# One buffer and four transfers for the queries of a unit, in place of three pieces and twelve

## The chip, the cores and the metric

The kernel runs on one core of a Trainium2 chip. The metric is the time of one launch in microseconds on the device, and the time of a version is the median of its runs. The core has five engines with an instruction queue each: TensorE (PE in the profile; its weight loads are PEld), VectorE (DVE), ScalarE (ACT), GpSimd (POOL) and SyncE (SP), which here only issues transfers (DMAs). An engine works through its own queue strictly in order, and engines wait for each other on semaphores.

## The reference

Two cross attention layers are applied one after the other to 32 sequences of 256 positions with 320 channels, with 77 context rows of 512 channels for each sequence. There are 20 heads of 16 channels. Cut to what is computed:

```python
def layer(x, ctx, Wq, Wk, Wv, Wo, bo):         # all float32
    q, k, v = heads(x @ Wq), heads(ctx @ Wk), heads(ctx @ Wv)
    s = einsum("bhqd,bhkd->bhqk", q, k) / sqrt(16)
    o = merge(einsum("bhqk,bhkd->bhqd", softmax(s), v))
    return o @ Wo + bo + x

x = layer(x, ctx, *L0)       # the object, others and ip parts of layer 0 have no rows here
x = layer(x, ctx, *L1)
```

## The kernel before

**Units.** Sixteen pairs of sequences times two layers make 32 units, in an order in which layer 0 runs four pairs ahead of layer 1 (`units_in_order`). Channels lie on partitions and positions along the free axis, so a pair's 320 x 512 values are 1280 columns (NX) of 128 partitions. The 20 heads of the two sequences form five groups of 256 columns; groups 0 to 3 are columns 0 to 1023, group 4 is the rest.

**What a unit does.** `keys` and `queries` (or `outputs_and_queries`, which also makes the outputs of the unit three before) project with TensorE; ScalarE copies the results to SBUF as `kR` and `q`. `mask_keys` makes `kT`. `maxima` computes scores once in order to find each row's maximum (TensorE writes `psm` at L500, VectorE reduces it at L512); `turn` lays these maxima out as rows, and SyncE moves them to `max_rows` (L537). `scores` computes the scores again, transposed, for the exponential: at L550 it puts the negative maxima into PSUM (`pss`), and at L558 it adds keys times queries. For accuracy these use a high and a low half of each number, made by `split` (L278 is the high half, L279 the low one). `products` and `divide` multiply with the values and normalise (`po` L578, `turned` L590, `normal` L599 on GpSimd), `turn_back` makes `oT`.

**The queries' halves.** The scores need the two heads of a pair on all partitions, and the high and low half of a head on neighbouring ones. `split_queries(u, i)` splits piece i of `q` into a buffer `halves`; `spread_queries(u, i)` moves it to `qs` with four DMAs (L316), one for each head e of a pair and each half h, each from 64 partitions to 64 others. The pieces are columns 0 to 511 (groups 0 and 1), 512 to 1023 (groups 2 and 3) and 1024 to 1279 (group 4); the `halves` tag has two buffers of 2 x 512 columns. So a unit has twelve such DMAs: eight of 128 KB and four of 64 KB. Unit 0 is split on VectorE, all others on GpSimd.

**Order.** The order is written out by hand. `at(slot, where, step)` files every step, and at the end the slots are gone through in order, and in each slot the places in a fixed order:

```python
order = (
    "load", "maxima", "turn back", "scores", "values", "rest", "back", "turn", "split", "full", "last",
)
```

`start(u)` is unit u's slot: 0, 5, 9, 13 and then the same 17 later, and so on. Unit u's first scores (group 0) stand in slot `start(u)`, except that the last unit's stand in `start(30) + 3`. Its pieces are split in slots `start(u-1) - 1`, `start(u-1)` and `start(u-1) + 1`, and spread at the head of `start(u-1)`, `start(u-1) + 1` and `start(u-1) + 2`. Every DMA but a few of the first weights is issued by SyncE in this order: loads of x (L120), contexts (L125, L426) and weights (L140), kS from `k_halves` (L290), v from `stage` (L480, L485), `max_rows` (L537), and the stores (L624, L643). A SyncE that waits for one of them holds all that follow.

**Buffers.** `ident`, a 128 x 128 identity, is a constant of its own; it is read once, at L178. `turned` has two buffers of 544 columns.

Of the kernel before, what the change touches and what calls it, by code (L numbers as in the profile page):

```python
# [52 lines left out]
F32 = mybir.dt.float32  # L53
F32R = mybir.dt.float32r
# [4 lines left out]
B, S, C, CA, L = 32, 256, 320, 512, 77  # L59
HEADS, HD = 20, 16  # L60
P = 128
NB = 2
NT = NB * S
NX = 2 * NT + S
# [31 lines left out]
def xattn_kernel(ctx: ExitStack, tc: tile.TileContext, xT, cT, cP, weights, outT):  # L96
    nc = tc.nc

    const = ctx.enter_context(tc.tile_pool(name="const", bufs=1))
    io = ctx.enter_context(tc.tile_pool(name="io", bufs=3))  # L100
    work = ctx.enter_context(tc.tile_pool(name="work", bufs=3))
# [11 lines left out]
    def load_x(p):  # L113
        x_sb = io.tile([P, NX], F32, tag="x", name=f"x_{p}", bufs=AHEAD + 2)
        xs[p] = x_sb
        if p == 0:
            for a, b in ((0, NT), (NT, 2 * NT), (2 * NT, NX)):
                nc.sync.dma_start(out=x_sb[:, a:b], in_=xT[p, :, a:b])
        else:
            (nc.scalar if p == 1 else nc.sync).dma_start(out=x_sb, in_=xT[p])  # L120

    def load_context(u):
        p = units[u][0]
        c_sb = cs[u] = io.tile([P, NKA, NB * L], F32, tag="c", name=f"c_{u}", bufs=3)
        nc.sync.dma_start(out=c_sb, in_=cP[:, p])  # L125
# [3 lines left out]
    for layer in range(2):  # L129
        wide = const.tile([P, WIDE], F32, name=f"w_{layer}")  # L130
        d = {"all": wide}
# [12 lines left out]
    first, _, _ = PARTS["q"]  # L144
    for i in range(2):
        n = slice(first + i * C, first + (i + 1) * C)
# [4 lines left out]

    ones = const.tile([P, P], F32, name="ones")
    nc.vector.memset(ones, 1.0)
    ident = const.tile([P, P], F32, name="ident")
    make_identity(nc, ident)


# [37 lines left out]
    st = [{} for _ in units]  # L195
# [80 lines left out]
    def split(engine, high, low, x):  # L276

        engine.tensor_copy(high, x)  # L278
        engine.tensor_tensor(low, x, high.bitcast(F32), ALU.subtract)  # L279

    def split_keys(u):

        split(nc.gpsimd if u else nc.vector, k_halves[:, :, 0], k_halves[:, :, 1], st[u].pop("kr"))
# [11 lines left out]
    PIECES = ((0, NT), (NT, 2 * NT), (2 * NT, NX))  # L295

    def split_queries(u, i):

        a, b = PIECES[i]
        x = st[u]["halves", i] = work.tile(  # L300
            [P, 2, NT], F32R, tag="halves", name=f"halves_{u}_{i}", bufs=2
        )
        split(
            nc.gpsimd if u else nc.vector, x[:, 0, : b - a], x[:, 1, : b - a], st[u]["q"][:, a:b]
        )

    def spread_queries(u, i):

        a, b = PIECES[i]
        if i == 0:  # L310
            st[u]["qs"] = work.tile([P, 2, NX], F32R, tag="qs", name=f"qs_{u}", bufs=2)
        to = st[u]["qs"].bitcast(F32).rearrange("(d h) e n -> h e d n", h=2)
        x = st[u].pop(("halves", i)).bitcast(F32).rearrange("(d e) h n -> e h d n", e=2)
        for e in range(2):
            for h in range(2):
                nc.sync.dma_start(out=to[h, e, :, a:b], in_=x[e, h, :, : b - a])  # L316

    def keys(u, t):
        p, layer = units[u]
        w, c_sb = w_sb[layer], cs[u]  # L320
        if t == 0:
            st[u]["kr"] = work.tile([P, NG, L], F32, tag="kR", name=f"kR_{u}", bufs=2)
        kR = st[u]["kr"]
        ps = bank(f"psk_{u}_{t}")
        for kc in range(NKA):
            by_columns(
                ps[:, 0 : 2 * L],
                w["k"][:, kc, t * P : (t + 1) * P],
                c_sb[:, kc, :],
                start=(kc == 0),  # L330
                stop=(kc == NKA - 1),
            )
        nc.scalar.copy(kR[:, 2 * t : 2 * t + 2].rearrange("p g k -> p (g k)"), ps[:, 0 : 2 * L])  # L333
        mask_keys(u, t)

    def keys_rest(u):

        p, layer = units[u]
        w, c_sb = w_sb[layer], cs[u]
        ps = bank(f"psk_{u}_2")  # L340
        for kc in range(NKA):
            for i in range(4):
                b, m = 1 - i // 2, i % 2
                nc.tensor.matmul(  # L344
                    ps[32 * i : 32 * i + 32, 0:L],
                    w["k"][:, kc, 2 * P + 32 * m : 2 * P + 32 * m + 32],
                    c_sb[:, kc, b * L : (b + 1) * L],
                    start=(kc == 0),
                    stop=(kc == NKA - 1),
                )  # L350
        nc.scalar.copy(st[u]["kr"][:, 4], ps[:, 0:L])
        mask_keys(u, 2)
# [70 lines left out]
    def load_chunk(layer, i):  # L423
        n = min(P, B * L - i * P)
        c_sb = cvs[layer, i] = io.tile([P, NKA, P], F32, tag="cv", name=f"cv_{layer}_{i}", bufs=3)
        nc.sync.dma_start(out=c_sb[:, :, :n], in_=cT[:, :, i * P : i * P + n])  # L426
# [180 lines left out]
    def values(u, g):  # L607
        st[u]["n", g] = divide(u, g, products(u, g))
# [47 lines left out]
    def at(slot, where, step):  # L656
        place.setdefault((slot, where), []).append(step)

    def start(u):

        return 17 * (u // 4) + (0, 5, 9, 13)[u % 4]
# [17 lines left out]
    for u, (p, layer) in enumerate(units):  # L679

        s = start(u - 2)
        if layer == 0 and u > 0:
            at(s - 5 - (u == 1), "load", lambda p=p: load_x(p))
        if u > 0:
            at(s - 4, "load", lambda u=u: load_context(u))
        if u > 1:
            k = (0, 1, 2) if u == 2 else (s - 2, s - 1, s + 1)
            at(k[0], "rest", lambda u=u: keys(u, 0))
            at(k[1], "rest", lambda u=u: keys(u, 1))
            at(k[2], "rest", lambda u=u: keys_rest(u))  # L690
        paired = u > 2 and u - 3 not in late
        if paired:
            at(s, "full", lambda u=u: outputs_and_queries(u - 3, u))
        elif u > 1:
            at(s, "last", lambda u=u: queries(u))
        if u > 1:
            at(s + 2, "split", lambda u=u: split_keys(u))
            at(start(u - 1), "load", lambda u=u: spread_keys(u))
            for i in range(3):
                at(start(u - 1) + i - 1, "split", lambda u=u, i=i: split_queries(u, i))  # L700
                at(start(u - 1) + i, "load", lambda u=u, i=i: spread_queries(u, i))
        need = range(p * NB * L // P, ((p + 1) * NB * L - 1) // P + 1)
        new = [i for i in need if i >= made[layer]]
        made[layer] += len(new)
        first = (-6, -2)[u] if u < 2 else start(u - 1) + 1
        slots = {}
        for k, i in enumerate(new):
            at(first - 3 - (u == 0) + k, "load", lambda layer=layer, i=i: load_chunk(layer, i))
            if i in few:
                slots[i] = first  # L710
                at(first, "full", lambda layer=layer, i=i: vals_of_few(layer, i))
                continue
            for h in range(2):
                slots[i] = first + (0 if u < 2 else k if len(new) > 1 else h)
                at(slots[i], "full", lambda layer=layer, i=i, h=h: vals(layer, i, h))
        for i in need:
            at(slots.get(i, first), "full", lambda u=u, i=i: place_vals(u, i))
        for g in range(NG):
            slot = slot_of(u, g)
            at(slot, "scores", lambda u=u, g=g: scores(u, g))  # L720
            at(slot + 1, "values", lambda u=u, g=g: values(u, g))
            if g < 4:
                at(slot + 2, "turn back", lambda u=u, g=g: turn_back(u, g))
            else:
                at(slot + 1, "back", lambda u=u, g=g: turn_back(u, g))
        if u == NU - 1:
            at(end, "full", lambda u=u: finish(u))
            at(end, "last", lambda u=u: finish_rest(u))
        if u in late:
            for t in range(2):  # L730
                at(late[u][t], "full", lambda u=u, t=t: finish(u, (t,)))
            at(late[u][2], "rest", lambda u=u: finish_rest(u))
            at(max(late[u]), "last", lambda u=u: store(u))
# [32 lines left out]
    at(-7, "split", lambda: split_keys(0))  # L766
    at(-6, "load", lambda: spread_keys(0))
    for i in range(3):
        at(-6 + i, "split", lambda i=i: split_queries(0, i))
        at(-5 + i, "load", lambda i=i: spread_queries(0, i))  # L770
    for slot, h, n in ((-6, 0, 3), (-6, 3, 3), (-4, 6, 2), (-4, 8, 2)):
        at(slot, "maxima", lambda h=h, n=n: maxima((0, h, n)))
    at(-4, "turn", lambda: turn(0))
# [1 line left out]
    at(-3, "split", lambda: split_keys(1))  # L775
    at(-2, "load", lambda: spread_keys(1))
    for i in range(3):
        at(-3 + i, "split", lambda i=i: split_queries(1, i))
        at(-2 + i, "load", lambda i=i: spread_queries(1, i))
    for slot, h, n in ((-2, 0, 3), (-2, 3, 2), (0, 5, 3)):  # L780
        at(slot, "maxima", lambda h=h, n=n: maxima((1, h, n)))
    at(1, "maxima", lambda: maxima((1, 8, 2), (2, 0, 1)))
# [118 lines left out]
```

## Time and profile before

| | |
|---|---|
| time, median of three runs | 944.42 us (943.32 to 945.34) |
| the profiled execution | 947.08 us, of which 945.3 us are the span of the instructions |
| busy: PE, PEld, DVE, ACT, POOL | 926.6, 640.8, 574.5, 432.0, 406.9 us |
| granted TensorE clock, mean | 0.998 |
| chain that ended last | PE 88%, DVE 7%, DMA 2%, SPq 1%, issue 1% |
| DMA packets | 114740, 133.03 MB |
| spread of the queries | 256 DMAs of 128 KB and 128 of 64 KB, median issue 587 ns |
| splits of the queries on GpSimd | high half 606 ns, low half 1277 ns for 512 columns |

A busy time is the union of an engine's instructions; PE includes what the model of the profile takes for the ends of its pipelined matmuls. A row of the waits names the engine and line that waited, who ended the wait, the total in us, the number of times and the longest. A row of the timeline has the start and the length in us, the engine, the line, the operation, what it writes and reads, and how many instructions were merged. SPq is SyncE's queue: the time there is that of issuing a DMA, not of moving its data. A row of the busy times by stretch has, for each engine, us and instructions, and at the end the granted clock of TensorE as a share, the mean share of the 16 DMA engines that was busy, and GB/s.

### The profile page before, as it was taken

Reading aid. Unit: us, or ns where it says so; the run is one execution under the profiler, and the core shown is the slowest. Engines: PE = TensorE matmul, PEld = TensorE weight load, DVE = VectorE, ACT = ScalarE, POOL = GpSimd, SP = SyncE. Lnnn points to the kernel's source line nnn. Section 1 sums busy time; section 2 is a strip of 40 time slices with the busy share of each in tenths; the row PEclk is TensorE's granted clock in tenths of the full one; section 3 lists DMA queues with packets and bytes.
Section 4 is the critical chain, followed back from the end, with each engine's and each line's share of the span. In section 5 each row is a group of like instructions: output and inputs, shape, how many; then the busy total and the mean of one; then the engine's idle time right before and its main releaser. Section 6 shows DMA issues by size and latency. Waiting matters only on the chain.

```text
span 945.3 us, 48848 instructions
## 1 busy us (share of the span) xinstructions
PE 926.6 (98%) x21582; PEld 640.8 (68%) x21582; DVE 574.5 (61%) x1330; ACT 432.0 (46%) x975; POOL 406.9 (43%) x608
## 2 busy tenths in 40 slices
PE   8999999999999999999999999999999999999998
PEld 6666667766667666666766677666767666676654
DVE  4475557655577565665656666665566654776575
ACT  2254443644435534355443545335454354444462
POOL 2354445434455434455234454344553335543431
PEclk9999999999999999999999999999999999999999
DMA  6664444253453525536245352355433543353342
GB/s 227 196 217 129 133 147 145 82 172 120 163 153 95 197 76 163 165 104 201 68 145 176 98 201 82 125 175 161 153 96 120 160 155 119 92 162 105 118 136 97
DMA packets 114740, 133.03 MB, mean 141 GB/s; under 512 B 47012, under 2 KB 76004, under 8 KB 114530
## 3 DMA queue, kind: packets, MB, share of 16 engines
q1 hardware_dynamic: 113666, 127.42, 42.8%
q8 instruction: 170, 2.79, 1.3%
q10 hardware_dynamic: 864, 2.49, 0.7%
q14 instruction: 40, 0.33, 0.1%
HBM read 35.39 MB, written 10.49 MB: 49 GB/s over the span
## 4 chain that ended last, share of the span: by engine, by line
PE 88%; DVE 7%; DMA 2%; SPq 1%; issue 1%; POOL 0%; ACT 0%; POOLq 0%
PE psy L203 15%; PE po L578 15%; PE psq L203 14%; PE psm L500 10%; PE psv L203 7%; PE pss L558 7%; PE psk L203 7%; PE psy L237 4%; PE pss L550 4%; PE psq L237 3%; DVE m L512 3%; DVE turned L590 1%; PE psk L344 1%; DVE maxes L533 1%; SPq L316 1%; DMA x<-in_xT_dram 1%
## 5 line engine op out<-in xcount | busy, mean ns | idle before, releaser
L564 ACT ACTIVATE pT<-pss 77x512 f32<-77x512 f32 x640 | 324.4, 593 | 171.7 <-PE pss L558 171.0
L512 DVE TENSOR_REDUCE m<-psm 128x6 f32<-128x462 f32 (+2 forms) x512 | 248.3, 551 | 221.4 <-PE psm L500 220.9
L599 POOL TENSOR_TENSOR normal<-turned,inv 128x256 f32<-128x256 f32 x160 | 99.3, 621 | 484.5 <-DVE inv L594 457.5
L578 PE MATMUL po<-pT,v 77*32 77x256 f32 x2560 | 166.8, 385 | 8.3 <-DVE m L512 5.2
L203 PE MATMUL psy<-oT,w 128*32 128x256 f32 (+1 forms) x3072 | 164.5, 379 | 0.0
L203 PE MATMUL psq<-x,w 128*32 128x256 f32 (+1 forms) x3072 | 153.4, 380 | 0.6 <-DMA w<-in_w_dram 0.6
L203 PEld LDWEIGHTS psy<-oT,w 128*32 128x32 f32 (+1 forms) x3072 | 88.4, 108 | 63.4 <-issue 15.2
L590 DVE STREAM_TRANSPOSE turned<-po 128x512 f32<-128x512 f32 x160 | 109.5, 684 | 24.4 <-PE po L578 24.3
L203 PEld LDWEIGHTS psq<-x,w 128*32 128x32 f32 (+1 forms) x3072 | 86.8, 109 | 54.9 <-issue 2.2
L274 POOL TENSOR_SCALAR kT<-kR,masks 128x154 f32<-128x154 f32 x186 | 113.3, 619 | 19.2 <-ACT kR L333 19.2
L578 PEld LDWEIGHTS po<-pT,v 77*32 77x32 f32 x2560 | 72.4, 109 | 69.6 <-DVE m L512 26.7
L500 PE MATMUL psm<-kT,q 32*128 32x154 f32 x2560 | 116.2, 306 | 2.3 <-POOL kT L274 2.0
L500 PEld LDWEIGHTS psm<-kT,q 32*128 32x128 f32 x2560 | 90.1, 183 | 35.3 <-issue 25.3
L279 POOL TENSOR_TENSOR halves<-q,halves 128x512 fp32r<-128x512 f32 (+1 forms) x93 | 102.1, 1098 | 7.8
L558 PE MATMUL pss<-qs,kS 32*77 32x256 f32 x2560 | 104.6, 276 | 0.0
L620 DVE SCALAR_TENSOR_TENSOR x<-psy,w,x 128x256 f32<-128x256 f32 x160 | 68.3, 476 | 50.6 <-PE psy L203 49.2
L558 PEld LDWEIGHTS pss<-qs,kS 32*77 32x77 f32 x2560 | 89.2, 141 | 11.3
L613 DVE STREAM_TRANSPOSE oT<-normal 128x256 f32<-128x256 f32 x160 | 67.0, 431 | 45.8 <-POOL normal L599 45.8
L203 PE MATMUL psv<-w,cv 128*32 128x160 f32 x2432 | 93.5, 299 | 0.2 <-DVE m L512 0.2
L418 ACT COPY q<-psq 128x256 f32<-128x256 f32 x28 | 10.4, 372 | 161.8 <-PE psq L237 161.8
L203 PEld LDWEIGHTS psv<-w,cv 128*32 128x32 f32 x2432 | 77.8, 110 | 4.4 <-DVE m L512 0.6
L550 PE MATMUL pss<-max_rows,less 32*77 32x512 f32 x640 | 78.7, 468 | 1.4 <-DMA max_rows<-mT 1.4
(48 smaller groups left out, 725.3 us busy)
## 6 DMA issues: line engine op xcount, KB each, us to landing
qs<-halves SPq DMA_DIRECT2D x256, 128.0 KB
kS<-k_halves SPq DMA_DIRECT2D x128, 192.5 KB
c<-in_cP_dram SPq DMA_DIRECT2D x32, 308.0 KB
cv<-in_cT_dram SPq DMA_DIRECT2D x38, 256.0 KB
out_dram<-x SPq DMA_DIRECT2D x15, 640.0 KB
x<-in_xT_dram SPq DMA_DIRECT2D x14, 640.0 KB
qs<-halves SPq DMA_DIRECT2D x128, 64.0 KB
v<-stage SPq DMA_DIRECT2D x26, 192.5 KB
```

Source lines behind the costliest of these rows:

```text
L203: nc.tensor.matmul(out[m : m + 32], lhsT[:, m : m + 32], rhs, **flags)
L274: engine.tensor_scalar_mul(kT[:, e], kR[:, groups], masks[:, e : e + 1])
L279: engine.tensor_tensor(low, x, high.bitcast(F32), ALU.subtract)
L500: nc.tensor.matmul(ps[j][:, i * 2 * L : (i + 1) * 2 * L], q[r, c * P : (c + 1) * P], kT[r, :, g % 2, :], start=True, stop=True,)
L512: nc.vector.tensor_reduce(st[u]["m"].rearrange("p e h j -> p h e j")[:, first : first + n, :, j], ps[j][:, at * 2 * L : (at + n) * 2 * L]. ...
L550: nc.tensor.matmul(ps[j][:L], less[r, g % 4, :], max_rows[u % 2][r, g // 4], start=True, stop=False)
L558: nc.tensor.matmul(ps[j][:L, e * S : (e + 1) * S], st[u]["ks"][r, e, g, half, :], q[r, :], start=False, stop=(half == 1 and e == 1),)
L564: nc.scalar.activation(st[u]["p", g][j][:L], ps[j][:L], AF.Exp, scale=SCALE)
L578: nc.tensor.matmul(po[o : o + 32, e * S : (e + 1) * S], vpad[:L, b, pair, e].rearrange("p a d -> p (a d)"), pT[j][:L, e * S : (e + 1) * S] ...
L590: nc.vector.transpose(turned[:, 0 : 2 * S], po)
L599: nc.gpsimd.tensor_tensor(normal.rearrange("p q e d -> p e q d"), outs, inv.unsqueeze(3).broadcast_to([P, 2, S // 32, HD]), ALU.mult,)
L620: nc.vector.scalar_tensor_tensor(x, ps[:, 0:S], w_sb[layer]["b"][:, 0, t : t + 1], x, ALU.add, ALU.add)
```

## The change

The three pieces of a unit now lie in one `halves` buffer of 2 x 1280 columns, of which there is one in place of two smaller ones. `split_queries` still splits piece by piece, in the same slots from unit 2 on, and now always on GpSimd. `spread_queries` runs once a unit, in the slot of the former third piece, and issues four DMAs of 1280 columns (320 KB). For units 0 and 1, all three pieces are split in the slot of the former first piece, and spread in the slot after. To make room, `ident` is allocated from the `turned` buffers.

```diff
-    ident = const.tile([P, P], F32, name="ident")
+    ident = work.tile([P, 2 * (S + HD)], F32, tag="turned", name="ident", bufs=2)[:, 0:P]
...
     def split_queries(u, i):
         a, b = PIECES[i]
-        x = st[u]["halves", i] = work.tile(
-            [P, 2, NT], F32R, tag="halves", name=f"halves_{u}_{i}", bufs=2
-        )
-        split(
-            nc.gpsimd if u else nc.vector, x[:, 0, : b - a], x[:, 1, : b - a], st[u]["q"][:, a:b]
-        )
-
-    def spread_queries(u, i):
-
-        a, b = PIECES[i]
         if i == 0:
-            st[u]["qs"] = work.tile([P, 2, NX], F32R, tag="qs", name=f"qs_{u}", bufs=2)
-        to = st[u]["qs"].bitcast(F32).rearrange("(d h) e n -> h e d n", h=2)
-        x = st[u].pop(("halves", i)).bitcast(F32).rearrange("(d e) h n -> e h d n", e=2)
+            st[u]["halves"] = work.tile(
+                [P, 2, NX], F32R, tag="halves", name=f"halves_{u}", bufs=1
+            )
+        x = st[u]["halves"]
+        split(nc.gpsimd, x[:, 0, a:b], x[:, 1, a:b], st[u]["q"][:, a:b])
+
+    def spread_queries(u):
+
+        qs = st[u]["qs"] = work.tile([P, 2, NX], F32R, tag="qs", name=f"qs_{u}", bufs=2)
+        to = qs.bitcast(F32).rearrange("(d h) e n -> h e d n", h=2)
+        x = st[u].pop("halves").bitcast(F32).rearrange("(d e) h n -> e h d n", e=2)
         for e in range(2):
             for h in range(2):
-                nc.sync.dma_start(out=to[h, e, :, a:b], in_=x[e, h, :, : b - a])
+                nc.sync.dma_start(out=to[h, e], in_=x[e, h])
...
             for i in range(3):
                 at(start(u - 1) + i - 1, "split", lambda u=u, i=i: split_queries(u, i))
-                at(start(u - 1) + i, "load", lambda u=u, i=i: spread_queries(u, i))
+            at(start(u - 1) + 2, "load", lambda u=u: spread_queries(u))
...
     for i in range(3):
-        at(-6 + i, "split", lambda i=i: split_queries(0, i))
-        at(-5 + i, "load", lambda i=i: spread_queries(0, i))
+        at(-6, "split", lambda i=i: split_queries(0, i))
+    at(-5, "load", lambda: spread_queries(0))
...
     for i in range(3):
-        at(-3 + i, "split", lambda i=i: split_queries(1, i))
-        at(-2 + i, "load", lambda i=i: spread_queries(1, i))
+        at(-3, "split", lambda i=i: split_queries(1, i))
+    at(-2, "load", lambda: spread_queries(1))
```

## The prediction

> **What bounds the kernel.** I read the page first, then TensorE's waits, then SyncE's issues beside TensorE's matmuls around the places where the moved transfers go.
>
> The page says that TensorE is the bound:
>
> ```profile
> PE 926.6 (98%) x21582; PEld 640.8 (68%) x21582; DVE 574.5 (61%) x1330; ACT 432.0 (46%) x975; POOL 406.9 (43%) x608
> ```
>
> Outside PE's 926.6 us there are 18.7 us of the 945.3 us span. A change to transfers and splits can therefore gain little; it can lose as much as it makes PE wait. PE's waits from 0 to 62 us:
>
> ```profile
> PE psm L500 <- POOL kT L274: 2.0, 1, 2.0
> PE pss L550 <- DMA max_rows<-mT: 1.4, 1, 1.4
> ...
> PE psk L203 <- DVE m L512: 0.5, 1, 0.5
> ```
>
> The columns are total, count, longest. All three have the queries' split and spread behind them: GpSimd made unit 2's kT late, because it had sat 4.70 us at L278 for a halves buffer; SyncE issued unit 0's max_rows only at 34.41 (mT was ready at 27.95), behind pieces 0 and 1 of unit 0's spread; VectorE spent 21.35 to 23.56 on two splits ahead of a reduction. From 62 to 890 us PE waits 5.0 us on DVE in ten places and on no DMA. The 2.0 us wait also costs clock. Busy time by stretch (PEclk, DMA share and GB/s are the last three columns):
>
> ```profile
> 48.70:50.75 2.05, 0.00 (x1) 0.00 (x1) 0.00 (x0) 0.00 (x0) 2.00 (x3) 1.00 0.54 176
> ...
> 51.40:54.80 3.40, 3.40 (x48) 2.00 (x44) 2.92 (x9) 2.04 (x4) 0.00 (x0) 0.50 0.78 233
> ```
>
> After 2.05 us of idleness PE ran 3.40 us at a granted clock of 0.50, worth 1.7 us of full speed.
>
> Next, the place that decides: SyncE's issues before unit 3's first scores, and those scores on PE.
>
> ```profile
> 115.55 2.71 SPq L537 DMA_DIRECT2D max_rows<-mT  x4
> 118.35 1.38 SPq L485 DMA_DIRECT2D v<-stage  x1
> 119.84 2.45 SPq L316 DMA_DIRECT2D qs<-halves  x4
> ```
>
> ```profile
> 123.08 0.46 PE L550 MATMUL pss<-max_rows,less 32*77 32x512 f32 x4
> 123.37 0.64 PE L558 MATMUL pss<-qs,kS 32*77 32x256 f32 x16
> ```
>
> L316 at 119.84 is piece 2 alone (group 4's queries). Group 0, read at 123.37, came with piece 0, issued at 98.10. After the change everything is issued where piece 2 is, 3.53 us before the first read. The last unit is worse:
>
> ```profile
> 909.33 2.72 SPq L537 DMA_DIRECT2D max_rows<-mT  x4
> 912.10 1.76 SPq L643 DMA_DIRECT2D out_dram<-x  x1
> 913.96 2.80 SPq L316 DMA_DIRECT2D qs<-halves  x4
> 916.86 1.74 SPq L485 DMA_DIRECT2D v<-stage  x2
> 918.70 2.79 SPq L480 DMA_DIRECT2D v<-stage  x4
> 921.59 1.18 SPq L316 DMA_DIRECT2D qs<-halves  x2
> ```
>
> ```profile
> 916.81 0.63 PE L558 MATMUL pss<-qs,kS 32*77 32x256 f32 x16
> ```
>
> Unit 31's piece 2 is issued 4.78 us after group 0 is read.
>
> **How long the four new DMAs take.** No DMA of that form is in the trace; its time T, from the first issue to the first reader, is built from rows. Unit 10's piece 2 was issued at 319.22 into idle engines; two stretches of one answer, one of another, and one line of the chain:
>
> ```profile
> 319.60:320.30 0.70, 0.70 (x22) 0.52 (x18) 0.70 (x3) 0.70 (x3) 0.41 (x1) 1.00 0.00 0
> 320.30:320.90 0.60, 0.60 (x28) 0.59 (x20) 0.60 (x2) 0.60 (x2) 0.00 (x0) 1.00 0.33 109
> ```
>
> ```profile
> 504.00:504.30 0.30, 0.30 (x16) 0.15 (x8) 0.30 (x2) 0.19 (x1) 0.30 (x1) 1.00 1.04 380
> ```
>
> ```profile
> 45.95 2.07 DMA qs<-halves
> ```
>
> First data moves 1.1 us after issue. With the engines full, SBUF-to-SBUF rows (kS there) move at 380 GB/s, so 4 x 320 KB = 1.31 MB needs 3.45 us; issuing, four times the median 0.587 us, is shorter. The chain's line is one 128 KB DMA, 2.07 us from issue to the waiting reader: 1.1, then 0.35 of data, leaves 0.6 for completion. T = 1.1 + 3.45 + 0.6 = 5.1 us. Below, T could be 4.5 (no completion lag); above, 6.3, since four issues of half the bytes (42.71 to 48.02) took 5.3 where others stood ahead.
>
> **Part by part.** *Twelve DMAs become four.* 8 x 32 issues of 0.587 us leave SyncE, 4.7 us a unit. Bytes stay; packets fall. PE waits on no spread now, so none of this is on the path after the start, except that SyncE is earlier where it ran without a break. Before most late issues it did not: ahead of 115.55 it sat idle for 9.4 us until VectorE's mT. The position does not move up.
>
> *Pieces 0 and 1 go later*, past SyncE's max_rows and v transfers. For each unit I took the start of piece 2's issue and group 0's first L558, the distance between them against T = 5.1. Units 1, 2, 5, 6, 9, 10, 13, 14, 17, 18, 21, 22, 25, 26, 29 and 30 have 7.2 to 14.8 us: nothing. The others, distance and stall: 3: 3.53, 1.6; 4: 4.62, 0.5; 7: 3.24, 1.9; 8: 4.68, 0.4; 11: 4.20, 0.9; 12: 4.95, 0.2; 15: 3.83, 1.3; 16: 4.12, 1.0; 19: 2.97, 2.1; 20: 4.51, 0.6; 23: 4.23, 0.9; 24: 4.16, 0.9; 28: 4.88, 0.2. Sum 12.5. Unit 27 is issued at 817.42, read at 816.87, behind six v transfers, with a first issue of 1.69 us instead of 0.59: 0.55 + 1.1 + 5.1 = 6.8. Unit 31: SyncE works without a break from 909.33, so the 2.85 us of piece 1 come off: issue 918.74, landed 923.84, read 916.81: 7.0. All this stands on PE, in order, nothing beside it: 26.3 us. Bounds: at T = 4.5 about 18, at 6.3 about 44.
>
> *Clock.* The row above took 1.7 us after 2.05 us idle; the 1.44 us idle at 38.5 was followed by a granted 1.00. Units 27 and 31 pay that surely, 19 perhaps: 3.4 (bounds 0 and 7). [...]
>
> *One halves buffer.* GpSimd's split of unit u+1 now waits for unit u's four DMAs; queued behind it are normal and kT, which VectorE's transposes and PE wait for. Unit 3: landed 124.9, next split 125.8, and that moves back with PE's stall. Unit 4: 154.7 against 155.9; unit 27: 824 against 819.3 plus 6.8. Cost taken: 0; bound 0.5 us for each of 15 units, 7. The waits of the two-buffer scheme (POOL's 12.0 us at L278) go.
>
> *Unit 0 on GpSimd, at once.* VectorE loses 2 x (0.42 + 0.69) + 0.29 + 0.43 = 2.9 us, of which 2.2 stood before a reduction. GpSimd gains 2 x (0.61 + 1.28) + 0.40 + 0.73 = 4.9 us. The cover is its 19.2 us of waiting up to 25.71; were it gone, unit 1's kT would be up to 4.9 late. The splits may slow VectorE's masks at 12 to 14 us; PE reads them from 15.9 on, so nothing.
>
> *The start.* Unit 0's four issues run 24.9 to 27.6, then c and w, so max_rows is issued near 29.7. Ahead of it lie 0.66 + 1.31 + 0.32 + 0.53 = 2.8 MB from 25 us on; at the 262 GB/s of 24 to 29 us they end at 35.7, and max_rows lands near 37; PE comes at 38.0. The 1.4 us go. Unit 1's splits run 32 to 37 instead of ending at 49.37, so unit 2's kT is masked at 43: the 2.05 and the 1.7 of clock go. With VectorE's 0.5 that is 5.7; I take 4.7, since something is next late (bounds 2 and 5.7).
>
> *ident in a turned buffer*: the same two GpSimd instructions, last read by VectorE at 2.2 us, long before the slot's next use: 0.
>
> **The sum.** 26.3 + 3.4 - 4.7 = +25.0. On the profiled execution (947.08, of which 945.3 span) 972.1; the median of the runs is 944.42, 0.3% under it, so 969.4.
>
> [...]
>
> **Rivals.** *Hidden (faster).* Fewer issues bring SyncE to the four DMAs early: from 2.2 us earlier in the regular units (T = 5.1 against unit 19's 2.97) and about 7 us in units 27 and 31, no stall is left and the start's 4.7 remains: 939.7. For it: SyncE loses a third of its issues. Against: the idle 9.4 us ahead of 115.55, which fewer issues don't shorten, and 3.45 us of data alone. 0.07. *Only the two big ones*: the small stalls are hidden because SyncE runs earlier, 27 and 31 remain: 6.8 + 7.0 + 3.4 - 4.7 = +12.5, 957; 0.11, of which 0.02 for the case that these two shrink as well and nothing measurable is left. *Congested*: T = 6.3, as with 42.71, and clock drops after several stalls: 44 + 7 - 3 = +48, 992; 0.14. *The change does not do what it says*: a 5120-byte row moved in several packets would make the engines slower; that ends in the congested case. *Start of unit 0 worse*: GpSimd's splits delay VectorE's masks by their 4.9 us; that turns the start from -4.7 to about 0 and is inside the range.
>
> **How the numbers follow.** Forecast 0.68: 969.4, its own range 957 to 983. Range 952 to 990: it takes in the two-big case and T up to about 6; left out are the hidden case and most of the congested one, below 0.2. A measurement of this kernel can tell about 0.2%, 1.9 us, from no change (its three runs span 2.0 us). Slower by more: 0.91; within: 0.02; faster: 0.07.
>
> **What would show it.** Right: waits "PE pss L558 <- DMA qs<-halves" near the 13 small times above, in units 3, 7, 19 the longest of them, and 6 to 7 us each at units 27 and 31; granted clock under 1 after those two; L316 x128 of 320 KB; packets 114740 - 32 x 8 x (64 + 16) = 94260; no PE wait for kT near 50 us; first scores at about 38 us. Wrong: PE still without DMA waits after 62 us (then the landing is faster than my rate, or SyncE earlier); or POOL L278 waiting for qs in most units, with PE late on kT or normal (then the single buffer, not the late issue, is the price).

## The result, and the profile after

The changed kernel takes 1046.53 us (median of 4 runs, 1042.8 to 1049.09), the one before 943.87 us (4 runs on the same chip, 943.26 to 945.34). The ratio is 1.108, 95% interval 1.104 to 1.112. The prediction said 969.4 us with a range of 952 to 990: the sign was right, the size a factor of four too small. The profiled execution took 1049.09 us, with a span of 1047.3 us: 102.0 us more than the span before.

The page of the kernel after, with TensorE's busy time, the packets and the transfers of the queries:

```profile
PE 965.0 (92%) x21582; PEld 651.9 (62%) x21582; DVE 575.4 (55%) x1324; ACT 432.6 (41%) x975; POOL 413.1 (39%) x614
...
DMA packets 94256, 132.98 MB, mean 127 GB/s; under 512 B 42916, under 2 KB 63716, under 8 KB 94050
...
qs<-halves SPq DMA_DIRECT2D x128, 320.0 KB
```

The change does what it says: 128 transfers of 320 KB, and 94256 packets where 94260 were forecast. PE does the same 21582 matmuls but is busy 38.4 us longer. TensorE's waits in the kernel after (who waited, for whom, total us, times, longest; lines from 316 on stand two lower than before, so L556 is the former L558):

```profile
PE pss L556 <- DMA qs<-halves: 57.2, 26, 7.5
PE po L576 <- DVE m L510: 6.3, 12, 1.0
PE pss L556 <- issue: 6.3, 6, 2.0
PE pss L556 <- DMA kS<-k_halves: 4.4, 2, 2.9
```

The waits for VectorE are as they were. New are 57.2 + 6.3 + 4.4 = 67.9 us at the first matmuls of scores. In the last row, units 16 and 19, the transfers of kS came last by the trace; SyncE issues them right behind the spread, and the spread's own last rows had landed only 1.0 and 0.6 us earlier. The start is better. The stretch from 0 to 62 us (columns: us, then busy time of PE, PEld, DVE, ACT and POOL; at the end granted clock, DMA share, GB/s), before and after:

```profile
0.00:62.00 62.00, 55.07 (x1202) 39.43 (x1206) 30.89 (x77) 17.52 (x45) 20.64 (x36) 0.97 0.66 212
```

```profile
0.00:62.00 62.00, 59.12 (x1366) 43.60 (x1370) 36.15 (x85) 22.24 (x55) 30.07 (x49) 1.00 0.71 243
```

PE's idle time in it fell from 6.9 to 2.9 us, and the 3.4 us at half clock are gone (1.7 us): 5.7 us gained. (Unit 1's first scores come 6.8 us earlier, at 60.5 in place of 67.2 us; what lies beyond the 5.7 is busy time and counted there.) The books close to 0.3 us: 67.9 of waits, plus 38.4 + 1.7 = 40.1 us that the same matmuls took longer at a lower clock (the 1.7 because the kernel before had some of that too), minus 5.7, is 102.3, where 102.0 were measured.

**The longest wait.** Unit 15 shows what was missed. SyncE's queue in the kernel after, in the order of issue:

```profile
488.19 2.45 SPq L483 DMA_DIRECT2D v<-stage  x3
490.73 4.05 SPq L314 DMA_DIRECT2D qs<-halves  x4
```

TensorE at that time (the bracket holds the idle time ahead of a matmul and what ended it):

```profile
494.65 0.46 PE L548 MATMUL pss<-max_rows,less 32*77 32x512 f32 x4
502.62 0.71 PE L556 MATMUL pss<-qs,kS 32*77 32x256 f32 x8 [7.52 <-DMA qs<-halves]
504.39 0.71 PE L556 MATMUL pss<-qs,kS 32*77 32x256 f32 x8 [1.05 <-DMA qs<-halves]
```

The transfers were issued 4.37 us before the scores came up; they took 11.9 us to the first reader, and 13.7 us to the heads e = 1. The time by stretch around it:

```profile
490.00:494.00 4.00, 3.99 (x104) 3.04 (x98) 2.10 (x4) 1.83 (x5) 3.16 (x5) 1.00 0.50 165
...
496.00:499.00 3.00, 0.00 (x0) 0.00 (x0) 0.45 (x1) 0.00 (x0) 1.43 (x3) 0.79 0.77 237
499.00:502.00 3.00, 0.00 (x0) 0.00 (x0) 0.00 (x0) 0.00 (x0) 0.00 (x0) 0.50 0.08 30
...
504.40:508.00 3.60, 3.60 (x45) 2.26 (x48) 0.00 (x0) 2.83 (x6) 1.80 (x2) 0.51 0.33 102
```

From 499 to 502 us every compute engine stands still, and the DMA engines are busy to 0.08, at 30 GB/s: of 16 engines little more than one is working (1/16 is 0.06). The last row shows the second half of the cost: PE is back at work, fully busy, at a granted clock of 0.51. What that one engine moves can be read from the transfers issued just before:

```profile
v<-stage SPq DMA_DIRECT2D x1, 182.5 KB
v<-stage SPq DMA_DIRECT2D x1, 137.5 KB
v<-stage SPq DMA_DIRECT2D x1, 55.0 KB
```

182.5 KB are 73 rows of 2560 bytes, 137.5 KB 55 rows, 55 KB 22 rows. In the trace's packets, once the other transfers are through, ten 2560-byte rows start per us, one after the other (0.102 us each), and then the 5120-byte rows of the spread, 0.2 us each. By that, 73 rows one after the other take 7.4 us. The spread's rows on that engine stand behind them: its last 16 rows start at 500.5 us and end 12.9 us after the issue, while all other rows of the spread had ended within 7.6 us of it.

How few engines carry a transfer's rows is in the trace too, in the events that report its landing: 16 for each transfer of the spread (64 rows), but one for these 73 rows, 11.0 us after their issue, and 11 each for the 22 and the 55. (A transfer of v with fewer than 16 has one more, 1.05 to 2.07 us after the issue, ahead of any landing.) In the traces before and after, the number is the same each time that a row count occurs: one for 23, 29, 31, 47, 53, 71 and 73 rows, two for 46 and 74, three for 51 and 57, four for 76. I read it as the number of engines; the DMA share of 0.08 of 16, at 30 GB/s, agrees with one. Of the spread's four transfers here, each had 15 of its 16 events by 498.9 us; the last ones came at 501.75, 502.54, 503.34 and 504.15. The number of rows is that of one sequence's context rows in a `stage` of 128, so it changes from unit to unit.

The kernel before has the same transfers, unit 15's among them. A stretch of its trace:

```profile
476.00:478.00 2.00, 2.00 (x44) 1.22 (x40) 0.45 (x1) 0.96 (x2) 0.94 (x2) 1.00 0.12 38
478.00:480.00 2.00, 2.00 (x60) 1.21 (x60) 0.35 (x1) 0.00 (x0) 0.81 (x2) 1.00 0.34 128
```

There too 38 GB/s with transfers queued, and PE busy throughout, since the piece on its way there was that of group 4, which is read last. The row could have been read before the change was made.

### The profile page after: what moved, and what is told of

Read it like the earlier page. It is cut to its first block, busy times and chain, and to the rows that moved or that the text cites. A ratio compares the mean times of both kernels' runs of the same rounds, so it can differ in the third digit from the quotient of the medians.

```text
span 1047.3 us, 48231 instructions
## 1 busy us (share of the span) xinstructions
PE 965.0 (92%) x21582; PEld 651.9 (62%) x21582; DVE 575.4 (55%) x1324; ACT 432.6 (41%) x975; POOL 413.1 (39%) x614
## 2 busy tenths in 40 slices
DMA packets 94256, 132.98 MB, mean 127 GB/s; under 512 B 42916, under 2 KB 63716, under 8 KB 94050
## 4 chain that ended last, share of the span: by engine, by line
PE 69%; DMA 10%; DVE 8%; SPq 5%; issue 4%; POOL 3%; ACT 0%; POOLq 0%; ACTq 0%
PE psy L203 15%; PE psq L203 13%; PE po L576 11%; DMA qs<-halves 9%; PE psm L498 6%; PE pss L556 6%; PE psv L203 4%; DVE m L510 4%; PE psy L237 4%; PE psk L203 3%; PE psq L237 3%; SPq L314 3%; PE pss L548 2%; DVE turned L588 2%; POOL kT L274 2%
## 5 line engine op out<-in xcount | busy, mean ns | idle before, releaser
L576 PE MATMUL po<-pT,v 77*32 77x256 f32 x2560 | 177.9, 406 | 9.2 <-DVE m L510 6.3
L556 PE MATMUL pss<-qs,kS 32*77 32x256 f32 x2560 | 117.4, 292 | 67.9 <-DMA qs<-halves 57.2
L203 PE MATMUL psy<-oT,w 128*32 128x256 f32 (+1 forms) x3072 | 177.9, 401 | 0.0
L556 PEld LDWEIGHTS pss<-qs,kS 32*77 32x77 f32 x2560 | 93.8, 150 | 88.5 <-DMA qs<-halves 45.3
L203 PEld LDWEIGHTS psy<-oT,w 128*32 128x32 f32 (+1 forms) x3072 | 92.7, 115 | 76.7 <-issue 32.5
L576 PEld LDWEIGHTS po<-pT,v 77*32 77x32 f32 x2560 | 74.9, 113 | 75.1 <-DVE m L510 26.2
L279 POOL TENSOR_TENSOR halves<-q,halves 128x512 fp32r<-128x512 f32 (+1 forms) x96 | 105.6, 1100 | 8.0
```

Of the source, the lines that this page charges most:

```text
L203: nc.tensor.matmul(out[m : m + 32], lhsT[:, m : m + 32], rhs, **flags)
L556: nc.tensor.matmul(ps[j][:L, e * S : (e + 1) * S], st[u]["ks"][r, e, g, half, :], q[r, :], start=False, stop=(half == 1 and e == 1),)
L576: nc.tensor.matmul(po[o : o + 32, e * S : (e + 1) * S], vpad[:L, b, pair, e].rearrange("p a d -> p (a d)"), pT[j][:L, e * S : (e + 1) * S] ...
```

## The experiments

Three theories. A: the late transfers of the queries queue behind v transfers that run on few DMA engines. B: the single `halves` buffer makes GpSimd wait (46.2 us at L278 in 15 places, 12.0 before), and what GpSimd makes is late. C: transfers of 320 KB are slow in themselves. The row of GpSimd in the kernel after:

```profile
POOL halves L278 <- DMA qs<-halves: 46.2, 15, 6.9
```

"Few" are below the nine units 11, 12, 15, 16, 22, 23, 24, 25 and 30, whose v transfers ahead of the spread, or one of them, run on one or two engines by the landing events above; "many" are 3, 4, 7, 8, 19, 20, 27, 28 and 31, what is left of the prediction's list, with three or more engines ahead, or no such transfer right ahead. Sums of waits at the first scores come from each kernel's trace, by unit. In the kernel after they are 42.3 us for the few and 25.1 for the many.

**v_even: the same late transfers, with v's rows cut for the engines.** Where the row count of a v transfer is over 16 and has no divisor from 8 to 16 (in the traces before and after, these counts are the ones with seven landing events or fewer), its rows are sent as a multiple of 16 and a rest.

```diff
-                nc.sync.dma_start(out=...[k0 - first : k1 - first, b], in_=...[k0 - i * P : k1 - i * P])
+                n = k1 - k0
+                engines = max(d for d in range(1, 17) if n % d == 0)
+                cut = k0 + 16 * (n // 16) if engines < 8 and n > 16 else k1
+                for r0, r1 in ((k0, cut), (cut, k1)):
+                    if r0 < r1:
+                        nc.sync.dma_start(out=...[r0 - first : r1 - first, b], in_=...[r0 - i * P : r1 - i * P])
```

> The changed kernel with one thing altered: a v<-stage transfer whose rows fall on fewer than 8 DMA engines (its row count has no divisor from 8 to 16) is cut into a part of 16, 32, 48 or 64 rows and a rest of at most 15 rows. Theory A (the late spread queues behind v rows that one or a few engines carry alone; 53, 73, 71 and 47 rows go through one engine in 5 to 7 us): no engine carries more than 5 rows of a v transfer, the spread lands about 5 us after its issue in every unit, PE waits about 15 to 30 us for it instead of 64, and the time is 960 to 985. Theory B (the single halves buffer holds GpSimd, 46 us at L278, and PE waits for what GpSimd makes late): no change, 1040 to 1050. Theory C (four DMAs of 320 KB are slow in themselves): no change, 1040 to 1050.

Measured: 1003.15 us, 1.0625 times the kernel before (1.0583 to 1.0668). 43 us of the 102 are gone by making v's transfers more numerous and nothing else. By unit, the few fell from 42.3 to 11.8 us and the many only from 25.1 to 23.2: the effect is where theory A puts it, and B and C, which expected no change, fall. The spread of the few lands 4.8 to 6.4 us after its issue, 7.0 to 14.1 in the changed kernel. No unit waits longer than 5.1 us now. GpSimd's waits at L278 fell from 46.2 to 13.0 us with them, so most of these came of the slow landing (L561 is L556 here):

```profile
PE pss L561 <- DMA qs<-halves: 30.4, 22, 3.9
```

```profile
POOL halves L278 <- DMA qs<-halves: 13.0, 9, 3.5
```

The time is above what A expected. The last row of a spread lands 4.5 to 6.7 us after the issue even so: in all 15 of units 1 to 31 where it takes over 6 us, a packet of an instruction fetch (16 KB, 0.9 to 1.5 us) starts between the spread's issue and its landing, 0.7 to 4.3 us after the issue; where it takes under 5, none does. No run removes these fetches, so that they cause it is not shown. And PE's busy time is still 949.2 us, 24 us of it clock.

**v_behind: the v transfers issued after the spread** in place of before it.

```diff
-            at(slots.get(i, first), "full", lambda u=u, i=i: place_vals(u, i))
+            if u > 1 and slots.get(i, first) == first:
+                at(start(u - 1) + 2, "load", lambda u=u, i=i: place_vals(u, i))
+            else:
+                at(slots.get(i, first), "full", lambda u=u, i=i: place_vals(u, i))
```

> The changed kernel with the order on SyncE altered: the v<-stage transfers that stood at the end of slot start(u-1)+1, ahead of the spread, now follow it at the head of slot start(u-1)+2. Theory A: the spread is issued 1 to 4 us earlier and has no long v rows ahead of it on any engine, landing about 4.7 us after issue; most stalls go: 940 to 965. Theory B: 1040 or so, since the spread still ends in the same slot. Theory C: about 1030, the 1 to 4 us earlier issue alone.

Measured: 981.77 us, ratio 1.0399 (1.0360 to 1.0438). Its waits on PE:

```profile
PE pss L556 <- DMA qs<-halves: 17.1, 15, 2.1
PE pss L548 <- ACT stage L440: 9.7, 4, 3.5
```

The few are down to 5.1 us, about as much as the prediction's list had for them, though not unit by unit; their spreads land 5.4 to 6.5 us after the issue. The many fell too, from 25.1 to 12.0 us. But without the v transfers ahead the spread is also issued earlier, by 0.3 to 8.1 us ahead of the scores among the few and 0.6 to 4.9 among the many; so this run alone does not separate the two, as v_even does. A's range of 940 to 965 was missed, and so were B's and C's figures. New is the second row: the `stage` buffer is read later, so ScalarE fills it late and PE, in order, waits for that.

**early4: the four transfers one slot earlier**, with the split of the third piece moved up to the second's slot.

```diff
-                at(start(u - 1) + i - 1, "split", lambda u=u, i=i: split_queries(u, i))
-            at(start(u - 1) + 2, "load", lambda u=u: spread_queries(u))
+                at(start(u - 1) + min(i, 1) - 1, "split", lambda u=u, i=i: split_queries(u, i))
+            at(start(u - 1) + 1, "load", lambda u=u: spread_queries(u))
```

> The changed kernel with the four DMAs one slot earlier: piece 2 is split in slot start(u-1) together with piece 1, and the spread stands at the head of slot start(u-1)+1, ahead of that slot's max_rows and v transfers. One buffer and four DMAs stay. Theory A: no PE wait for qs is left, and the start's gain (unit 2's first scores 6.8 us earlier) remains: 936 to 942. Theory B: still over 1000, since the buffer is still single. Theory C: the same as A, since there is time to hide them.

Measured: 949.49 us, ratio 1.0059 (1.0039 to 1.0079). This is the change with all but the late issue: one buffer, four transfers of 320 KB, unit 0 at once. B, which expected over 1000 us, does not reach beyond what is left here. C expected the same as A here; it is v_even that speaks against C. Of the 34 waits at the first scores two remain, both in unit 31, of 2.2 and 1.4 us, followed by 3.4 us at half clock. These 5.3 us are most of what the time lies above A's range:

```profile
PE pss L556 <- DMA qs<-halves: 3.6, 2, 2.2
```

**late12: late, but in twelve transfers** of the three pieces.

```diff
...
-        for e in range(2):
-            for h in range(2):
-                nc.sync.dma_start(out=to[h, e], in_=x[e, h])
+        for a, b in (PIECES[i] for i in pieces):
+            for e in range(2):
+                for h in range(2):
+                    nc.sync.dma_start(out=to[h, e, :, a:b], in_=x[e, h, :, a:b])
```

> The changed kernel with the spread cut into pieces again, twelve DMAs, but all issued where the four are: late, from one buffer. Groups 0 and 1 then wait for the first four DMAs (128 KB each) alone. Theory A: these land about 3.6 us after the first issue plus the wait behind the v rows, so the short stalls shrink by about 1.5 us each and those behind 47 to 73 rows on one engine stay; issuing all takes 7 us, so groups 2 to 4 may wait in their turn: 990 to 1030. Theory C: about 950. Theory B: 1040 or more.

Measured: 1042.51 us, ratio 1.1042 (1.1000 to 1.1085). Its time is as bad as that of the change, in part by another way; A's range of 990 to 1030 was missed, and B's "1040 or more" met:

```profile
PE pss L558 <- DMA qs<-halves: 33.6, 21, 6.3
PE psy L203 <- DVE oT L613: 21.6, 12, 2.8
```

```profile
POOL halves L278 <- DMA qs<-halves: 83.0, 17, 8.8
```

Piece 0 comes first now, so that the scores wait half as long; but the last of twelve issues is later, the buffer is free later, and here GpSimd's wait (83.0 us) does reach PE: `normal` stands behind the split on GpSimd, `oT` behind `normal`, and PE waits 21.6 us for it. Each of these 12 waits of PE ends 3.1 to 3.2 us after a wait of GpSimd at L278 has ended. This is B's path, and it carries about a third of the time that PE lost in waits.

**early12: one buffer, twelve transfers, each piece in its slot of before.** It differs from the kernel before in the one buffer, and in the start. `spread_queries` is as in late12, called for each piece:

```diff
-            at(start(u - 1) + 2, "load", lambda u=u: spread_queries(u))
+                at(start(u - 1) + i, "load", lambda u=u, i=i: spread_queries(u, (i,)))
```

> One halves buffer of 1280 columns as in the changed kernel, and its start; but the twelve DMAs of three pieces, each piece issued in the slot it had before. Theory A (the late issue, behind v transfers that run on one to three DMA engines, is what costs): nothing is late any more, PE waits under 2 us on qs, PE busy about 927, the start keeps its gain of 5 to 6 us: 937 to 942 us, ratio 0.993 to 0.998. Theory B (the single buffer is what costs, through GpSimd, which waits at L278 for the DMAs that read it): GpSimd waits at L278 as in the changed kernel (46 us) and PE gets late outputs: above 1000 us.

Measured: 959.83 us, ratio 1.0158 (1.0140 to 1.0176). Both theories missed. No wait on `qs` is left at the scores, as A said, but the span is 12.6 us longer than before. TensorE's and GpSimd's waits:

```profile
PE psy L203 <- DVE oT L613: 7.5, 4, 3.3
...
PE pss L550 <- DMA max_rows<-mT: 4.3, 1, 4.3
```

```profile
POOL halves L278 <- DMA qs<-halves: 13.0, 5, 4.5
```

Two things, then. One is a cost, the buffer: 9.0 us of waits at oT and x, and two more stretches at half clock, by which PE is busy 3.1 us longer than before. Around 480 us GpSimd stands 4.53 us at L278 until the transfers of unit 15's last piece have landed, which were issued at 468.95 right behind the same 73 rows of v and landed at 479.8; `normal` is late behind it, and PE waits 3.31 us for `oT`. Each of the four waits for `oT` ends 3.1 us after a wait of GpSimd at L278 has ended. That is B's path, fed by A's cause in this place; the other three were not followed back to their transfers. The other is a gain that did not come, at the start: unit 0's twelve issues hold SyncE, and the maxima are issued after them. SyncE's queue in early12:

```profile
23.81 9.60 SPq L316 DMA_DIRECT2D qs<-halves  x12
...
35.65 2.71 SPq L537 DMA_DIRECT2D max_rows<-mT  x4
```

In the changed kernel the issue in the same place, of four transfers, takes 3.37 us from 23.80 on, and max_rows is issued at 29.50. So the gain at the start is that of fewer issues; with twelve in the same place next to nothing of it is left (PE idle 7.1 us from 0 to 62 us, 6.9 before, and the same 3.4 us of half clock).

**late_few_engines and late_many_engines: early4, with nine units late each.** This puts the two halves of the loss into kernels of their own.

```diff
+            late_unit = u in (11, 12, 15, 16, 22, 23, 24, 25, 30)      # or (3, 4, 7, 8, 19, 20, 27, 28, 31)
             for i in range(3):
-                at(start(u - 1) + i - 1, "split", lambda u=u, i=i: split_queries(u, i))
-            at(start(u - 1) + 2, "load", lambda u=u: spread_queries(u))
+                slot = start(u - 1) + (i if late_unit else min(i, 1)) - 1
+                at(slot, "split", lambda u=u, i=i: split_queries(u, i))
+            at(start(u - 1) + (2 if late_unit else 1), "load", lambda u=u: spread_queries(u))
```

> Early issue as in early4, but units 11, 12, 15, 16, 22, 23, 24, 25 and 30 issue late, as in the changed kernel: the nine whose late DMAs stand behind v transfers of 74, 53, 73, 23, 73, 46, 47, 71 and 71 rows, which run on one or two DMA engines. My forecast's list has 0.9 + 0.2 + 1.3 + 1.0 + 0.9 + 0.9 = 5.2 us of stalls for them (22, 25 and 30: nothing): over early4's 949.5 about 955. Theory A (the rows queue on one engine in front of the spread's rows): about 42 us of stalls and 15 to 25 us of half clock: 995 to 1015 us.

> Early issue as in early4, but units 3, 4, 7, 8, 19, 20, 27, 28 and 31 issue late, as in the changed kernel: the nine units of my forecast's list whose v transfers ahead run on three or more engines, or have none right ahead. The forecast's list has 1.6 + 0.5 + 1.9 + 0.4 + 2.1 + 0.6 + 6.8 + 0.2 + 7.0 = 21.1 us of stalls for them, less early4's 3.6 at unit 31, and 2 us of clock beyond early4's: about 969. Theory A agrees on the stalls (25 us in the changed kernel) and adds clock, since every unit's stall of 2 us or more is followed by half clock: 975 to 992 us. That few-engine rows do not matter: the same as the run with the other nine late.

Measured: 1015.76 us (ratio 1.0751, 1.0722 to 1.0779) with the few late, 982.56 us (1.0399, 1.0373 to 1.0425) with the many late. A's range was missed by 0.8 us in the first and met in the second; the 955 and 969 us of the forecast's list are not, nor is "the same" for both. TensorE's first row of waits in the one, and the first two in the other:

```profile
PE pss L556 <- DMA qs<-halves: 43.6, 19, 7.5
```

```profile
PE pss L556 <- DMA qs<-halves: 18.7, 12, 4.1
PE pss L556 <- issue: 6.5, 4, 2.7
```

By unit, the few wait 42.2 us here (and unit 31, as in early4, 2.8) and 42.3 in the change; the many 25.3 here and 25.1 there. PE's busy time is 952.4 and 940.8 us, against 926.8 in early4. Over early4 the two cost 66.3 and 33.1 us, together 99.4, against 97.0 for all late units at once: the loss is the sum of its units. The same number of late units costs twice as much where the v rows go to one or two engines.

**early4_last: early4, and the last unit one slot earlier still**, all its splits at once.

```diff
             for i in range(3):
-                at(start(u - 1) + i - 1, "split", lambda u=u, i=i: split_queries(u, i))
-            at(start(u - 1) + 2, "load", lambda u=u: spread_queries(u))
+                slot = start(u - 1) - 1 + (0 if u == NU - 1 else min(i, 1))
+                at(slot, "split", lambda u=u, i=i: split_queries(u, i))
+            at(start(u - 1) + (u < NU - 1), "load", lambda u=u: spread_queries(u))
```

> The early issue of the four DMAs (as in the run early4, 949.5 us), and for unit 31 alone all splits and the issue one slot earlier still, so that the only wait on qs that was left there (2.2 + 1.4 us at unit 31, then 3.4 us at a clock of 0.50) goes. Theory A: that is 3.6 + 1.7 = 5.3 us less: 942 to 946 us, ratio 0.998 to 1.002, no PE wait on qs over 0.5 us. Theory B (single buffer): the wait turns up elsewhere, POOL L278 or PE L203, and the time stays at 948 to 951.

Measured: 941.62 us (median of 10 runs, 941.04 to 942.81) against 944.97 for the kernel before (15 runs, 942.78 to 946.72), ratio 0.9969 (0.9959 to 0.9980). It beats both kernels, by about 0.3% the one before. All TensorE waits of 0.5 us and over in it:

```profile
PE po L576 <- DVE m L510: 6.4, 12, 1.0
PE warm L193 <- DVE ones L153: 1.0, 1, 1.0
PE psq L237 <- issue: 0.7, 1, 0.7
PE pss L548 <- DMA max_rows<-mT: 0.5, 1, 0.5
```

No wait on `qs` is left, PE is busy for 925.2 us and the granted clock is 1.00 from 6 us to the end. The span is 4.3 us under that of before: 2.9 us less idle time of PE and 1.4 us less busy time (most of it the 1.7 of half clock). In the 15 runs of the kernel before the mean granted clock is 0.996 to 1.000, in the ten here it is 1.000.

## Why the prediction was wrong, point by point

| term | predicted, us | measured in the kernel after, us |
|---|---|---|
| waits of the nine "many" units | 21.1 | 25.1 |
| waits of the nine "few" units | 5.2 (22, 25 and 30: nothing) | 42.3 |
| other units | 0 | 0.5 |
| clock | 3.4 | 40.1 |
| one halves buffer | 0 (bound 7) | no row of its own on PE |
| start | -4.7 | -5.7 |
| not itemised | 0 | -0.3 |
| sum | +25.0 | +102.0 |

**The place and the mechanism of the waits held.** The late transfers are read too early, PE waits for them in order, and the bytes, packets, first scores (about 38 us forecast, 36.0 measured for the first pss) and the missing wait for kT near 50 us came as forecast. The distances from issue to first read were read rightly: in the 13 units with small stalls they changed by -0.4 to +0.5 us.

**T was right for empty engines and wrong as a constant.** Unit 31 has no slow v rows right ahead: data from 1.19 to 4.55 us after the issue, readers of the heads e = 1 at 4.98; forecast 1.1, 4.55 and 5.1. The step that failed is "With the engines full, SBUF-to-SBUF rows (kS there) move at 380 GB/s", taken for every unit: in unit 31, with no slow rows right ahead, it came out, but in unit 15 the last 16 rows moved on one engine at about 25 GB/s, and the readers waited for them. What stood ahead was charged only to SyncE's issue time ("past SyncE's max_rows and v transfers"), not to the engines. The bounds of T, 4.5 and 6.3, came from rows of one kind; the last packets of the nine few landed 7.0 to 14.1 us after the issue. So 22, 25 and 30 were put under "nothing" because 7.2 us looked like enough, and they waited 4.9, 3.4 and 2.8. That this is the cause is shown by taking the slow rows away (v_even: 42.3 to 11.8). Taking them out of the way agrees (v_behind: 5.1, part of it by an earlier issue), and so do the kernels with nine late units each.

**Among the many**, units 27 and 31 were over-charged (6.8 and 7.0; measured 5.4 and 4.8). For 27 the slow first issue of 1.1 us did not occur; for 31 the issue came 0.5 us behind the waiting matmul, not 1.9. In both, PE did the half of group 0 whose two transfers came first (about 0.7 us) before it waited for the other half. Units 4 and 8, with 51 rows on three and 76 on four engines ahead, were under-charged (0.5 and 0.4; measured 2.0 and 2.7), and so was 19 (2.1; measured 4.2, with an instruction fetch among its last packets). The errors partly cancelled.

**The clock term was the second miss, and as large as the first.** It was charged for two waits, at 1.7 us each. In the trace after there are 14 stretches at a granted 0.50, of 3.41, 6.83 or 10.24 us, 99 us in all (PE's waits included); the same matmuls took 40.1 us longer. So many follow from so many waits; but the price per wait was too small as well, since the row of 2.05 us idle that it came from is the smallest case. In late_many_engines, whose 25.3 us of waits are close to the 26.3 forecast, the clock took 940.8 - 926.6 + 1.7 = 15.9 us, not 3.4, and its 982.56 us is about what the change would have taken with waits as forecast: inside the range, and 13 us above the forecast.

The expectation of late_many_engines has half clock behind every stall of 2 us and over. In the trace after, it came with 14 of the 16 units that waited so long; units 7 (2.48 us) and 20 (2.03 us) had none. The lengths of the stretches are multiples of 3.41 us; what idle time stood ahead of them is in the last section.

**One halves buffer**: zero was right for the change as made, for a reason that the prediction did not give. GpSimd did wait (46.2 us), but PE was waiting for the same transfers already: 14 of GpSimd's 15 waits end within 0.1 us of one of PE's. With nothing late at the scores, in early12, the buffer cost PE 9.0 us at oT and x, and clock on top.

**The start** came out as reasoned: 5.7 us, its upper bound, and it needs the four transfers (early12 has next to none of it).

**The rivals.** "Congested" (992) came nearest, with T up to 6.3 and a clock that drops after several stalls; it took the right direction at too small a size, and for waiting packets in general, not for one engine. "Hidden" failed where the prediction said it would: fewer issues did not bring the late ones forward (by 0.5 us at most in the 13 units above). "Only the two big ones" had the two wrong: the big ones were 15, 24, 27 and 12.

## What to carry to other kernels

Here the transfers that were moved later were not only later by their issue: they queued, engine by engine, behind what was issued ahead, and the same 1.31 MB took 12.9 us behind 73 rows on one engine (unit 15) and 4.55 us with no such rows right ahead (unit 31). So look at each transfer ahead for how many engines it uses, and take the time of the fullest engine, not the bytes over the full rate. In the profile, a stretch with transfers queued and a DMA share little over 1/16 (0.08 and 0.12 here) is that sign, and it can be read before the change, where it is still hidden. Fewer, larger transfers paid here only when issued long enough ahead of the first read: the same four transfers cost 11% in the third slot, and one slot earlier (two for the last unit) they save 0.3%. And where PE is the bound, charge its waits for the clock too: of the 11 of 2 us and over in the trace after, ten ended within or just ahead of a stretch at half clock, and the clock cost 40 us on top of 68.

## What the runs showed of the hardware that was not expected

**A transfer of 73 rows held up those issued behind it.** 73 rows of 2560 bytes, at 0.102 us each, are about 7.4 us on one engine, and the spread issued behind them (unit 15) landed 12.9 us after its issue, against 4.55 us in unit 31, which had none right ahead.

**Half clock came after less than 3.41 us of idle time, by where it fell.** In each trace all changes of the granted clock lie on a grid of 3.413 us. Laid on that grid, PE's idle share in a window goes with the clock of the next. Over seven traces (before, after, early4, early12, v_even and the two with nine late units): of 1849 windows at full clock with under 30% of idle time none was followed by half clock, of 31 with 30 to 50% five were, of 37 with over half 36 were. Windows already at half clock stayed there in all 29 cases with 10% of idle time and over. So a wait of 2 us can cost clock or not by where it falls in the grid: in the trace after, the 2.03 us up to 665.62 were followed by none, and 0.88 and 1.17 us of idle time together, between 148.98 and 151.49, by 3.4 us at half clock. It can also last: in that trace the waits of 3.9 us and over were followed by 6.8 to 10.2 us.
